# A fused attention and mixture-of-experts kernel: heads shifted by half a block, half maxima, and another order of the first loads

## The chip, the cores and the metric

The kernel runs on one core of a Trainium2 chip. The metric is device time in microseconds, the median of several executions. The core's engines work side by side, each through its own list of instructions in order, and wait for one another by semaphores: TensorE (PE, matmuls; PEld are its weight loads), VectorE (DVE), ScalarE (ACT), GpSimd (POOL) and SyncE (SP, which issues most transfers).

## What is computed

Two layers over eight images of 256 channels by 1024 pixels, all in float32. The part that the change touches is the attention of layer 0, with eight heads of 64 channels and a softmax over the queries (axis 1), not over the keys:

```python
qkv = (xt @ w_qkv + b_qkv).reshape(B, S, N_HEADS, 3 * D_K)
q, k, v = jnp.split(qkv, 3, axis=-1)
attn = jnp.einsum('bihd,bjhd->bijh', q, k) * SCALE
attn = jax.nn.softmax(attn, axis=1)
res = jnp.einsum('bijh,bjhd->bihd', attn, v).reshape(B, S, N_HEADS * D_K)
res = res @ w_out + b_out + xt
```

Layer 1 then normalizes the tokens, adds a second attention of one head over 256 channels, normalizes again, and adds a mixture of eight experts, of which each token uses the two best.

## The kernel before

**Stages.** The images are worked through one after the other. For each: `values` (v for all heads, tile pv, L260), `layer0` (projection of q and k, scores and sums, then the output projection pr, L345), `attend` (second attention) and `dispatch` (choice of experts; token rows are scattered into a DRAM table `rows`). The experts run once for images 0 to 6 as one group, ahead of image 7, and once for image 7 at the end. The results of the first group (`results`: gathers of the experts' rows, tile yk, weighted sums, transposes pout, output) are put between the head pairs of image 7.

**A step of layer 0.** Heads are taken in four pairs g, keys in eight blocks j of 128. For a step (g, j) `head_scores` computes, for both heads, a score tile psc of 128 keys by 1024 queries, in two matmuls of 512 queries each (L282). The contraction is over 64 channels, so that head 0 uses the upper and head 1 the lower 64 rows of the array. Keys lie on the partitions, so the softmax over queries runs along a row: DVE takes the negated maximum of 1024 elements (nmax, L287), ACT the exponential with its row sum (ex, sums, L289), DVE the reciprocal (rs, L294) and v scaled by it (vs, L296). `head_values` adds vs times ex into two sums po (L306), again with the two heads side by side. One profile record of a float32 matmul is half of it: a matmul has two records.

**What sets the order.** The kernel is written in a tile framework. A scheduler places the instructions on each engine and adds the semaphore waits that the reads and writes of tiles call for. Score tiles, projections and transposes share one pool of three PSUM buffers of 128 x 1024 (`ps_big`); the sums and other small results share two of 128 x 512 (`ps_acc`). The sums of step j come after the scores of step j + 1. The projections of a pair (pqk, L241, evicted by DVE at L249) stand ahead of its first step.

**Loads.** SP loads w_qkv as six transfers that put q, k and v apart, in runs of 64 elements (L89), then the first image (L81), the biases and w_out, then fills `rows` with zeros (L491, eight transfers of 8 MB). POOL's queue loads three small weights and copies the experts' weights into one packed table `wpack` in DRAM (L164 to L175). The image b + 1 is loaded when image b begins.

Of the kernel before, what the change touches and what calls it, by code (L numbers as in the profile page):

```python
# [10 lines left out]
F32 = mybir.dt.float32  # L11
I32 = mybir.dt.int32
AF = mybir.ActivationFunctionType
ALU = mybir.AluOpType
# [4 lines left out]
def kernel(  # L19
# [41 lines left out]
    one = ctx.enter_context(tc.tile_pool(name="one", bufs=1))  # L61
    two = ctx.enter_context(tc.tile_pool(name="two", bufs=2))
    four = ctx.enter_context(tc.tile_pool(name="four", bufs=4))
    small = ctx.enter_context(tc.tile_pool(name="small", bufs=6))
    rowp = ctx.enter_context(tc.tile_pool(name="rowp", bufs=3))
    keep = ctx.enter_context(tc.tile_pool(name="keep", bufs=8))
# [12 lines left out]
    def load_x(b):  # L79
        xT = two.tile([P, NCC, S], F32, tag="xT", name=f"xT_{b}")  # L80
        nc.sync.dma_start(xT, x[b].rearrange("(cc p) s -> p cc s", p=P))  # L81
        return xT


    wqkv = const.tile([P, NCC, 3, INNER], F32, name="wqkv")
    w_src = w_qkv.rearrange("(cc p) (h t d) -> p cc t h d", p=P, t=3, d=DK)
    for t in range(3):
        for cc in range(NCC):
            nc.sync.dma_start(  # L89
                wqkv[:, cc, t, :].rearrange("p (h d) -> p h d", d=DK), w_src[:, cc, t]  # L90
            )
    next_x = load_x(0)
    b_src = b_qkv.rearrange("(h t d) -> t h d", t=3, d=DK)
    b_rows = two.tile([NPAIR, 2, P], F32, tag="xb", name="b_rows")
    for t in range(2):
# [57 lines left out]
    later = const.tile([P, E, NT], F32, name="later")  # L153
    nc.gpsimd.memset(later, 1.0)
    nc.gpsimd.memset(later[:, :, 0:1], 0.0)
    zero = one.tile([P, 2 * D], F32, tag="n", name="zero")
    nc.gpsimd.memset(zero, 0.0)

    wpack = dram.tile([E * P, WROW], F32, name="wpack")
    wp = wpack.rearrange("(e p) c -> e p c", p=P)
    for dc in range(NCC):
        nc.gpsimd.dma_start(  # L164
            wp[:, :, ts(dc, FF)], w1.rearrange("e (dc p) f -> dc e p f", p=P)[dc]
        )
    for fc in range(NFC):
        at = NCC * FF
        nc.gpsimd.dma_start(
            wp[:, :, at + fc * D : at + (fc + 1) * D],  # L170
            w2.rearrange("e (fc p) d -> fc e p d", p=P)[fc],
        )
    at = NCC * FF + NFC * D + NFC
    for e in range(E):
        nc.gpsimd.dma_start(wp[e, :, at : at + D], b2[e].partition_broadcast(P))  # L175
    wbs = [const.tile([P, WROW], F32, name=f"wb_{i}") for i in range(NWB)]


# [14 lines left out]
    for dc in range(NCC):  # L193
# [4 lines left out]
    nc.tensor.transpose(ps[:, : E * NFC], b1_rows, ident[: E * NFC, : E * NFC])  # L198
    b1T = const.tile([P, E * NFC], F32, name="b1T")
    nc.vector.tensor_copy(b1T, ps[:, : E * NFC])  # L200
    at = NCC * FF + NFC * D
    nc.sync.dma_start(
        wpack.rearrange("(e p) c -> p e c", p=P)[:, :, at : at + NFC],
        b1T.rearrange("p (e fc) -> p e fc", fc=NFC),
    )

    def bcast(t, n):

# [18 lines left out]
    def to_channels(t, dst, name):  # L227

        for cc in range(NCC):
# [2 lines left out]
                nc.tensor.transpose(pt[:, ts(i, P)], t[:, i, ts(cc, P)], ident)  # L232
            nc.vector.tensor_copy(dst[:, cc, :], pt)


    def project(b, xT, g, t):

        pq = big(f"pqk_{b}_{g}_{t}")
        for cc in range(NCC):
            for n in range(NH2):  # L240
                nc.tensor.matmul(  # L241
                    pq[:, ts(n, 512)],
                    wqkv[:, cc, t, ts(g, P)],
                    xT[:, cc, ts(n, 512)],
                    start=(cc == 0),
                    stop=(cc == NCC - 1),
                )
        dst = two.tile([P, S], F32, tag=f"qk{t}", name=f"qk{t}_{b}_{g}")
        nc.vector.tensor_scalar(  # L249
            dst, pq, b_qk[:, t, g : g + 1], SCALE if t == 0 else 1.0, ALU.add, ALU.mult  # L250
        )
        return dst
# [15 lines left out]
                nc.vector.tensor_add(v[:, i + j, :], pv[:, ts(j, 512)], b_v)  # L268
        return v

    def head_scores(b, g, j, q, k, v):


        sums = small.tile([P, 2], F32, tag="sums", name=f"sums_{b}_{g}_{j}")
        exps = []
        pss = []
        for h in range(2):
            pss.append(big(f"psc_{b}_{g}_{j}_{h}"))
        for n in range(NH2):
            for h in range(2):  # L280
                r = slice(h * DK, (h + 1) * DK)
                nc.tensor.matmul(  # L282
                    pss[h][:, ts(n, 512)], k[r, ts(j, P)], q[r, ts(n, 512)], start=True, stop=True
                )
        for h in range(2):
            nmax = small.tile([P, 1], F32, tag="nmax", name=f"nmax_{b}_{g}_{j}_{h}")
            nc.vector.tensor_reduce(nmax, pss[h], AX.X, ALU.max, negate=True)  # L287
            ex = four.tile([P, 1024], F32, tag="exps", name=f"ex_{b}_{g}_{j}_{h}")
            nc.scalar.activation(  # L289
                ex, pss[h], AF.Exp, bias=nmax, scale=1.0, accum_out=sums[:, h : h + 1]  # L290
            )
            exps.append(ex)
        rs = small.tile([P, 2], F32, tag="rs", name=f"rs_{b}_{g}_{j}")
        nc.vector.reciprocal(rs, sums)  # L294
        vs = four.tile([P, 2, DK], F32, tag="vs", name=f"vs_{b}_{g}_{j}")
        nc.vector.tensor_mul(  # L296
            vs,
            v[:, j, ts(g, P)].rearrange("p (h d) -> p h d", d=DK),
            rs.unsqueeze(2).to_broadcast([P, 2, DK]),
        )  # L300
        return exps, vs

    def head_values(j, exps, vs, po):
        for n in range(NH2):
            for h in range(2):
                nc.tensor.matmul(  # L306
                    po[n][h * DK : (h + 1) * DK, :],
                    vs[:, h, :],
                    exps[h][:, ts(n, 512)],
                    start=(j == 0),  # L310
                    stop=(j == NT - 1),
                )

    def layer0(b, xT, between):
        v = values(b, xT)
        res = one.tile([P, NPAIR, S], F32, tag="res", name=f"res_{b}")
        pending = None

        def finish(g, j, exps, vs, po):
            head_values(j, exps, vs, po)  # L320
            if j == NT - 1:
                for n in range(NH2):
                    nc.scalar.copy(res[:, g, ts(n, 512)], po[n])

        for g in range(NPAIR):
            q = project(b, xT, g, 0)
            k = project(b, xT, g, 1)
            po = None
            for j in range(NT):
                exps, vs = head_scores(b, g, j, q, k, v)  # L330
                if pending is not None:
                    finish(*pending)
                if po is None:
                    po = [acc(f"po_{b}_{g}_{n}") for n in range(NH2)]
                pending = (g, j, exps, vs, po)
            for group, item in between[g]:
                results(group, [item])
        finish(*pending)


        t1 = one.tile([P, NT, C], F32, tag="t1", name=f"t1_{b}")
        for i in range(NT):
            pr = acc(f"pr_{b}_{i}")
            for g in range(NPAIR):
                nc.tensor.matmul(  # L345
                    pr[:, :C], res[:, g, ts(i, P)], wo[:, g, :], start=(g == 0), stop=False
                )
            for cc in range(NCC):
                nc.tensor.matmul(
                    pr[:, ts(cc, P)], xT[:, cc, ts(i, P)], ident, start=False, stop=(cc == NCC - 1)  # L350
                )
            nc.vector.tensor_add(t1[:, i, :], pr[:, :C], b_o)
        return t1


    def attend(b, t1):
# [20 lines left out]
        def scores(i):  # L377
            psc = big(f"ps1_{b}_{i}")
            for ec in range(NCC):
                for n in range(NH2):  # L380
                    nc.tensor.matmul(  # L381
                        psc[:, ts(n, 512)],
                        xa[:, ec, ts(i, P)],
                        nT[:, ec, ts(n, 512)],
                        start=(ec == 0),
                        stop=(ec == NCC - 1),
                    )
            nmax = small.tile([P, 1], F32, tag="nmax", name=f"nmax1_{b}_{i}")
            nc.vector.tensor_reduce(nmax, psc, AX.X, ALU.max, negate=True)  # L389
            ex = four.tile([P, 1024], F32, tag="exps", name=f"ex1_{b}_{i}")  # L390
            ssum = small.tile([P, 1], F32, tag="ssum", name=f"ssum_{b}_{i}")
            nc.scalar.activation(ex, psc, AF.Exp, bias=nmax, scale=1.0, accum_out=ssum)  # L392
            return ex, ssum
# [81 lines left out]
    class Group:  # L475


        def __init__(self, n, items):
# [7 lines left out]
            self.counts = None  # L486
            self.kept = {}

            per = E * self.cap // (2 * P)
            for c in range(0, per, 32):  # L490
                nc.sync.dma_start(  # L491
                    self.rows.rearrange("(p c r) d -> p c (r d)", p=P, r=2)[:, c : c + 32],
                    zero.unsqueeze(1).to_broadcast([P, 32, 2 * D]),
                )

    def dispatch(b, t2, group):

# [271 lines left out]
                nc.scalar.copy(oT, pt)  # L769
                nc.sync.dma_start(out[b, ts(cc, P), :], oT)  # L770

    groups = [Group(n, items) for n, items in enumerate(GROUPS)]
    waiting = []
    for b in range(B):
        group = next(g for g in groups if b in g.items)
# [58 lines left out]
```

## Time and profile before

| quantity | value |
|---|---|
| runs | 3018.35 us median of 3 (3017.9 to 3022.67) |
| profiled execution, its own time | 3014.45 us |
| its span | 3012.4 us |
| mean granted clock of TensorE | 0.943 of full speed |
| q1, hardware queue | 123.62 MB |
| q0, software queue | 83.87 MB |

The profile page gives, for one execution, the busy time of each engine, its share of the span and its number of instructions; then the span in 40 slices of about 75 us, with PEclk for the clock that was granted to TensorE. The chain that ended last is followed back from the last instruction to what released each. In the groups, `out<-in` names the tiles, `xN` counts instructions, and the two numbers behind the bar are busy time and mean nanoseconds of one. In the timeline each row is start, length, engine, line and operation; the bracket at its end is the engine's idle time before it, and what ended it. A busy PE may still wait inside: the end of a matmul is modelled, and matmuls overlap.

### The profile page before, as it was taken

What the parts mean: (1) busy time and instruction counts of PE and PEld (TensorE: products, weight loads), DVE (VectorE), ACT (ScalarE), POOL (GpSimd) and SP (SyncE); (2) the same over time, 40 slices, a digit from 0 to 9 for tenths busy, and PEclk for the clock granted to TensorE, in tenths of its full rate; (3) what the DMA queues carried; (4) which work ended last, traced back from release to release, by engine and by line L of the source; (5) the groups of instructions that cost most, each with busy time, mean ns of one, the idle gap of its engine ahead of it and who ended that gap; (6) DMA issues with size and microseconds to landing.
All of it is one profiled execution on the core that took longest, in us unless ns stands there. A gap on an engine that the chain in (4) does not pass through costs nothing.

```text
span 3012.4 us, 26498 instructions
## 1 busy us (share of the span) xinstructions
PE 2698.4 (90%) x10049; PEld 1421.2 (47%) x10049; DVE 1476.6 (49%) x2662; ACT 843.1 (28%) x1448; POOL 451.4 (15%) x458
## 2 busy tenths in 40 slices
PE   5999899989998999899989999999679997778946
PEld 2336433653365336533553355335467773234534
DVE  2554555445645554555445544654523335555422
ACT  1451145114511441144114411442112112333101
POOL 1000200020002000200010001000144433441043
PEclk9999999999999999999999999999789998889967
DMA  9980100010001000000000000000055542332044
GB/s 318 386 323 14 42 1 0 15 42 1 1 14 39 4 1 14 35 8 1 14 32 11 0 15 28 14 1 1 29 175 184 185 137 71 118 118 68 0 157 159
DMA packets 92456, 209.19 MB, mean 69 GB/s; under 512 B 23504, under 2 KB 24168, under 8 KB 90280
## 3 DMA queue, kind: packets, MB, share of 16 engines
q1 hardware_dynamic: 59928, 123.62, 11.4%
q0 software_dynamic: 32400, 83.87, 9.0%
q8 instruction: 79, 1.29, 0.2%
q14 instruction: 49, 0.40, 0.0%
HBM read 113.22 MB, written 126.36 MB: 80 GB/s over the span
## 4 chain that ended last, share of the span: by engine, by line
PE 71%; issue 13%; DVE 6%; DMA 4%; ACT 4%; POOL 1%; SPq 0%; ACTq 0%; POOLq 0%; DVEq 0%
PE psc L282 18%; PE po L306 15%; PE py L403 8%; PE pqk L241 7%; PE ps L381 6%; PE pv L260 4%; PE pr L345 4%; PE pt_n L232 2%; PE px L366 2%; DMA yk<-y,yat 2%; PE pa L398 2%; ACT ex L289 1%; PE pe L718 1%; PE pl L427 1%; DVE nmax L287 1%
## 5 line engine op out<-in xcount | busy, mean ns | idle before, releaser
L289 ACT ACTIVATE ex<-psc,nmax 128x1024 f32<-128x1024 f32 x512 | 570.3, 1115 | 706.3 <-DVE nmax L287 697.0
L282 PE MATMUL psc<-qk,qk 64*128 64x512 f32 x2048 | 654.7, 628 | 38.3 <-DVE qk L249 21.5
L287 DVE TENSOR_REDUCE nmax<-psc 128x1 f32<-128x1024 f32 x512 | 604.3, 1219 | 137.7 <-PE psc L282 130.9
L306 PE MATMUL po<-ex,vs 128*64 128x512 f32 x2048 | 530.1, 618 | 18.0 <-DVE vs L296 18.0
L282 PEld LDWEIGHTS psc<-qk,qk 64*128 64x128 f32 x2048 | 266.7, 189 | 417.4 <-issue 284.8
L567 POOL TENSOR_TENSOR t<-t,n 128x2048 f32<-128x2048 f32 x8 | 36.1, 4508 | 1980.0 <-issue 1559.9
L306 PEld LDWEIGHTS po<-ex,vs 128*64 128x64 f32 x2048 | 130.6, 138 | 384.9 <-issue 205.2
L403 PE MATMUL py<-n,aT 128*128 128x256 f32 x1024 | 236.5, 384 | 11.2 <-DVE aT L400 11.2
L241 PE MATMUL pqk<-xT,wqkv 128*128 128x512 f32 x512 | 239.6, 618 | 2.3 <-DVE qk L249 2.3
L381 PE MATMUL ps<-nT,xa 128*128 128x512 f32 x512 | 236.8, 592 | 0.0
L403 PEld LDWEIGHTS py<-n,aT 128*128 128x128 f32 x1024 | 190.4, 190 | 67.4 <-DVE aT L400 43.8
L294 DVE RECIPROCAL rs<-sums 128x2 f32<-128x2 f32 x256 | 42.1, 165 | 288.1 <-ACT ex L289 287.8
L260 PE MATMUL pv<-wqkv,xT 128*128 128x512 f32 x256 | 139.0, 695 | 32.5 <-DMA xT<-in_x_dram 32.5
L718 PE MATMUL pe<-wb,hb 128*128 128x256 f32 x624 | 155.2, 392 | 13.6 <-ACT hb L703 13.4
L392 ACT ACTIVATE ex<-ps,nmax 128x1024 f32<-128x1024 f32 x64 | 71.3, 1114 | 332.7 <-DVE nmax L389 325.0
L241 PEld LDWEIGHTS pqk<-xT,wqkv 128*128 128x128 f32 x512 | 97.6, 197 | 127.2 <-issue 124.2
L693 PE MATMUL ph<-xb,wb 128*128 128x256 f32 x624 | 151.7, 386 | 3.1 <-DVE xb L685 3.1
L560 POOL DMA_INDIRECT rows<-n,d_at x128 | 124.9, 976 | 180.3 <-DVE row L547 128.4
L750 POOL DMA_INDIRECT yk<-y,yat x128 | 123.4, 964 | 179.0 <-DVE o L756 117.4
L703 ACT ACTIVATE hb<-ph,wb 128x256 f32<-128x256 f32 x156 | 65.5, 471 | 283.9 <-issue 237.6
L408 DVE SCALAR_TENSOR_TENSOR t<-py,rs,t 128x256 f32<-128x256 f32 x64 | 30.9, 483 | 228.2 <-PE py L403 228.2
L249 DVE TENSOR_SCALAR qk<-pqk,b_qk 128x1024 f32<-128x1024 f32 x64 | 82.1, 1283 | 119.7 <-PE pqk L241 119.7
(151 smaller groups left out, 2374.6 us busy)
## 6 DMA issues: line engine op xcount, KB each, us to landing
rows<-zero SPq DMA_DIRECT2D x8, 8192.0 KB, 51.1
y<-yb SPq DMA_DIRECT2D x78, 256.0 KB, 2.3
xT<-in_x_dram SPq DMA_DIRECT2D x8, 1024.0 KB, 5.1
sums<-t SPq DMA_DIRECT2D x8, 1024.0 KB, 3.9
o<-sums SPq DMA_DIRECT2D x8, 1024.0 KB, 6.7
out_dram<-oT SPq DMA_DIRECT2D x16, 512.0 KB, 7.6
wpack<-in_L_ffn_w_dram POOLq DMA_DIRECT2D x4, 1024.0 KB, 19.2
rows<-n,d_at POOLq DMA_INDIRECT x128, 2.4
```

The source lines that it names most:

```text
L241: nc.tensor.matmul(pq[:, ts(n, 512)], wqkv[:, cc, t, ts(g, P)], xT[:, cc, ts(n, 512)], start=(cc == 0), stop=(cc == NCC - 1),)
L260: nc.tensor.matmul(pv[:, ts(j, 512)], xT[:, cc, ts(i + j, P)], wqkv[:, cc, 2, :], start=(cc == 0), stop=(cc == NCC - 1),)
L282: nc.tensor.matmul(pss[h][:, ts(n, 512)], k[r, ts(j, P)], q[r, ts(n, 512)], start=True, stop=True)
L287: nc.vector.tensor_reduce(nmax, pss[h], AX.X, ALU.max, negate=True)
L289: nc.scalar.activation(ex, pss[h], AF.Exp, bias=nmax, scale=1.0, accum_out=sums[:, h : h + 1])
L306: nc.tensor.matmul(po[n][h * DK : (h + 1) * DK, :], vs[:, h, :], exps[h][:, ts(n, 512)], start=(j == 0), stop=(j == NT - 1),)
L381: nc.tensor.matmul(psc[:, ts(n, 512)], xa[:, ec, ts(i, P)], nT[:, ec, ts(n, 512)], start=(ec == 0), stop=(ec == NCC - 1),)
L403: nc.tensor.matmul(py[:, :D], aT[:, ts(m, P)], n1[:, m, :], start=(m == 0), stop=(m == NT - 1))
L560: nc.gpsimd.indirect_dma_start(out=view[:, :], out_offset=bass.IndirectOffsetOnAxis(ap=at[:, i : i + 1], axis=0), in_=n2[:, i, :], in_offs ...
L693: nc.tensor.matmul(ph[:, ts(fc, BR)], wb[:, dc * FF + fc * P : dc * FF + (fc + 1) * P], xb[:, dc, :], start=(dc == 0), stop=(dc == NCC - 1),)
L718: nc.tensor.matmul(py[:, ts(r, D)], hT[:, fc, ts(r, P)], wb[:, at + fc * D : at + (fc + 1) * D], start=(fc == 0), stop=(fc == NFC - 1),)
L750: nc.gpsimd.indirect_dma_start(out=yk[:, :], out_offset=None, in_=group.y[:, :], in_offset=bass.IndirectOffsetOnAxis(ap=ats[k][:, i : i + ...
```

## The change

Five edits go together.

1. **Order of the steps.** The steps of all four pairs form one list of 32. In an iteration, PE takes the first half of head 0 of this step, then the second half of head 1 of the step before, then the second half of head 0, then the first half of head 1. The sums follow two steps behind (`LAG = 2`). The exponentials get a pool of six buffers of their own.
2. **Maxima in halves.** The maximum of the first 512 queries is taken when these are there. For the other 512 an instruction multiplies by -1, takes the minimum with the first result and accumulates the minimum over the row; its full output goes into a tile `scrap` that nobody reads.
3. **Projections.** Those of the next pair are put behind steps 3 and 5 of the present pair.
4. **First loads.** The first image and w_qkv are loaded first, in whole rows, by four transfers; six copies on ACT and DVE then put q, k and v apart.
5. **Zeros and packed weights.** The zero fills and the copies into `wpack` all go through SP, behind the first k eviction. The zeros come from a DVE memset of a buffer that the experts use later.

```diff
-        for h in range(2):
-            nmax = small.tile([P, 1], F32, tag="nmax", name=f"nmax_{b}_{g}_{j}_{h}")
-            nc.vector.tensor_reduce(nmax, pss[h], AX.X, ALU.max, negate=True)
...
+        def first_max(at, h):
+            g, j = steps[at]
+            nmax = small.tile([P, 1], F32, tag="nmax1", name=f"nmax1_{b}_{g}_{j}_{h}")
+            nc.vector.tensor_reduce(nmax, pss[at, h][:, ts(0, 512)], AX.X, ALU.max, negate=True)
+            nmaxes[at, h] = nmax
+        def soften(at, h):
...
+            nc.vector.tensor_scalar(
+                scrap, ps[:, ts(1, 512)], -1.0, nmaxes.pop((at, h)),
+                ALU.mult, ALU.min, accum_out=nmax,
+            )
+            ex = expp.tile([P, 1024], F32, tag="exps", name=f"ex_{b}_{g}_{j}_{h}")
+            nc.scalar.activation(
+                ex, ps, AF.Exp, bias=nmax, scale=1.0, accum_out=sums[at][:, h : h + 1]
+            )
...
+        for at in range(last + LAG + 1):
+            if at <= last:
+                score(at, 0, 0)
+            if 0 < at <= last + 1:
+                score(at - 1, 1, 1)
+                soften(at - 1, 1)
+            if at <= last:
+                first_max(at, 0)
+                score(at, 0, 1)
+                score(at, 1, 0)
+                soften(at, 0)
+                first_max(at, 1)
+            if at >= LAG:
+                gather_values(at - LAG)
+            if at <= last:
+                g, j = steps[at]
+                if j == NT - 1:
+                    for group, item in between[g]:
+                        results(group, [item])
+                if g + 1 < NPAIR and j in (3, 5):
+                    if j == 3:
+                        qks.append([])
+                    qks[g + 1].append(project(b, xT, g + 1, len(qks[g + 1])))
```

`score(at, h, n)` is the matmul of L282 for head h and half n; `gather_values` is the former `head_values` with the copy of finished sums. The loads:

```diff
-    for t in range(3):
-        for cc in range(NCC):
-            nc.sync.dma_start(
-                wqkv[:, cc, t, :].rearrange("p (h d) -> p h d", d=DK), w_src[:, cc, t]
-            )
-    next_x = load_x(0)
+    for cc in range(NCC):
+        nc.sync.dma_start(next_x[:, cc, :], x[0, ts(cc, P), :])
+        nc.sync.dma_start(w_raw[:, cc, :], w_qkv[ts(cc, P), :])
+    for t in (2, 0, 1):
+        for cc in range(NCC):
+            copy = nc.scalar.copy if cc == 0 else nc.vector.tensor_copy
...
+    def prepare():
+        zero = wbs[0][:, : 2 * D]
+        with tc.issue_after(evicted[0, 0, 1].ins):
+            nc.vector.memset(zero, 0.0)
...
+        first = fill(groups[0])[0]
+        with tc.issue_after(first.ins):
+            pack()
+            for group in groups[1:]:
+                fill(group)
```

## The prediction

> **What bounds the kernel now.** I read the engine totals first, then the clock slices, the chain that ended last, the costly groups, and at last the timeline of one step of the convolution attention.
>
> ```profile
> span 3012.4 us, 26498 instructions
> ...
> PE 2698.4 (90%) x10049; PEld 1421.2 (47%) x10049; DVE 1476.6 (49%) x2662; ACT 843.1 (28%) x1448; POOL 451.4 (15%) x458
> ...
> PE psc L282 18%; PE po L306 15%; PE py L403 8%; PE pqk L241 7%; PE ps L381 6%; PE pv L260 4%; PE pr L345 4%; PE pt_n L232 2%; PE px L366 2%; DMA yk<-y,yat 2%; PE pa L398 2%; ACT ex L289 1%; PE pe L718 1%; PE pl L427 1%; DVE nmax L287 1%
> ```
>
> TensorE (PE) looks busy 90% of the span, and the two groups that the change rebuilds, the scores psc and the sums po, lead the chain. "Busy" hides small stalls, though, so I look at the pieces of the chain:
>
> ```profile
> 422.30 2.22 PE psc L282 x8
> 424.53 1.87 PE po L306 x8
> 426.39 2.42 PE psc L282 x7
> 428.81 1.87 PE po L306 x8
> ...
> 439.05 7.06 PE pqk L241 x16
> 446.11 1.86 PE po L306 x6
> 447.98 1.92 PE psc L282 x8
> ```
>
> A step is one psc block (4 matmuls, 8 records, the two heads side by side in the array) and one po block. With no stall it takes 1.92 + 1.87 = 3.79 us; in the steady state two steps take 2.22 + 1.87 + 2.42 + 1.87 = 8.38, so 4.19 each. What sets the 4.19 is the timeline's ring through two engines:
>
> ```profile
> 126.28 0.29 DVE L296 TENSOR_TENSOR vs<-v,rs 128x128 f32<-128x128 f32 x1
> 126.49 2.35 DVE L287 TENSOR_REDUCE nmax<-psc 128x1 f32<-128x1024 f32 x2
> ...
> 127.80 1.11 ACT L289 ACTIVATE ex<-psc,nmax 128x1024 f32<-128x1024 f32 x1 [1.75 <-DVE nmax L287]
> ...
> 128.93 1.11 ACT L289 ACTIVATE ex<-psc,nmax 128x1024 f32<-128x1024 f32 x1
> ...
> 130.17 0.17 DVE L294 RECIPROCAL rs<-sums 128x2 f32<-128x2 f32 x1 [1.33 <-ACT ex L289]
> 130.37 0.29 DVE L296 TENSOR_TENSOR vs<-v,rs 128x128 f32<-128x128 f32 x1
> 130.76 2.36 DVE L287 TENSOR_REDUCE nmax<-psc 128x1 f32<-128x1024 f32 x2
> ```
>
> max, exp, exp, reciprocal, scaled v, next max: DVE idles 1.33 us in front of rs. Stalled time to be won is thus 0.40 us in most steps, plus about 2 us at each change of head pair (psc piece of 3.76). In image 1 this stage runs from the projection at 353.5 to the first pr at 528.8: 175.3 us.
>
> **The change: the new step.** Lag 2 and the half-block shift break that ring: rs and vs are needed only a step later. But the built program's order shows a new wait. On PE a step is now: A = [head 0, first half, step s; head 1, second half, step s-1], B = [head 0, second half, s; head 1, first half, s], then po of s-2. The first matmul of B waits for DVE, for the half-maximum of the first half of the same score tile, although it writes the other half. Queued behind it on PE are B's second matmul and all of po; on DVE the second-half maxima wait for them. I price this ring from rows of before:
>
> - A: first pass to second, 0.53 (first psc block: weight loads at 57.79, 58.32, 58.75, 59.18).
> - Last pass to the start of the maximum: 59.81 - 59.18 = 0.63.
> - The half-maximum: L287 takes 1.219 for 1024 elements, L443 0.225 for 64, about 1.04 ns per element, so 0.69 for 512.
> - DVE end to PE start: 0.06 (L249 starts 56.45, takes 1.28; psc at 57.79).
> - B: 0.53 to its second pass, and from the last pass to po 0.53 (an unstalled block is 1.92, its last pass starts after 1.39).
> - po to the next block: 1.87.
>
> Sum 4.84 us. It would be 3.79 without the wait. Break-even comes below.
>
> What else could set the step? DVE: first max starts at A+1.16; head 1's min-accumulate at A+1.8; head 0's after B, at A+3.07; then the other first max, rs, vs. With the min-accumulate at S us the next first max (A+6.0) is late only if 3.07 + S + 0.63 + 0.5 > 6.0, S > 1.8. No row shows S: L268 (512 elements out of PSUM) is 0.68, L249 (1024, same instruction without the accumulator) 1.28. Below 0.68 nothing changes either, since the ring does not run through it; I take 0.75, the form of L249 at half length. ScalarE: two exps end about A+5.06, and B of the next step needs one at A+6.7. Both covered; if the cover went, the step would grow by the excess.
>
> The Trainium skill (VectorE: DVE Perf Modes, "Two Vector instructions with no wait between them") says that an op that also writes its accumulator is two instructions. For DVE no row shows it, for ScalarE one does: ACTIVATION_READ_ACCUMULATOR, 194 ns. By it S would be near 0.95 and the sum the same.
>
> **Projections** move out of the pair change, to after steps 3 and 5. Each is half of 7.06, 3.53, plus 0.08 for one more block change. In the next step DVE evicts first (1.28), so first max starts 0.15 later: 3.76 each. Pair change stalls go.
>
> One image: first pair's projections and eviction 7.06 + 1.43; two steps without po to fill the pipe about 6.8; 30 x 4.84 = 145.2; 6 x 3.76 = 22.6; at the end a last half score, max, exp, rs, vs and po, about 5.8. Sum 188.9, against 175.3: **+13.6 us an image**. Seven images +95. In image 7 the results of the first seven lie between the pairs, and 31.8 us pass from the first pout (2541.0) to the next psc (2572.8), of which gathers, not PE, set most. The projection leaves that hole and two score steps come in, of about its length; I take +14 there too, bounded by 0 (the scores hide fully) and +35 (7 us of projection at three pair changes now uncovered, on top).
>
> **Head.**
>
> ```profile
> 0.81 6.78 SPq L89 DMA_DIRECT2D wqkv<-in_L_conv_w_qkv_dram  x6
> ...
> 32.48 2.04 PE L260 MATMUL pv<-wqkv,xT 128*128 128x512 f32 x2 [32.48 <-DMA xT<-in_x_dram]
> ```
>
> The first real matmul waits for xT while the copies into wpack (POOL's queue) and wqkv in pieces of 256 B share the DMA engines: xT, 1 MB, took 24.7 us to land here, 5.1 in the median. Now x and w_qkv go first, in whole rows, and the wpack copies move behind. 2.5 MB at 1 MB per 5.1 us is 12.8, plus 0.8 to issue, plus a copy of at most 0.69 (as L268) before the last operand: 14.3. Bounds: 2 us faster (three landings overlap), or 6 slower if the small packets of W_rows, b_v and wo stand between. **-18**, range -12 to -20. Six w copies on ACT and DVE: two of them on the path, counted; the others lie under pv's 17 us. On SP the x of image 1 is now ahead of the zero fills; the fills start after the first k eviction, near 40 us instead of 31.5, and the twelve small wpack transfers, off POOL's queue, come behind seven of them. The fills took until about 215 us (slices of 386, 323, then 14 GB/s), and the first scatter comes after 348: some 100 us of cover; without it the scatter would wait. The zeroing moves to DVE, one instruction of about 0.5 us, under psc. Six exps buffers, the renamed tags and Group's move cost nothing: no wait on them is listed.
>
> **Sum.** Profiled execution 3014.45 + 95 + 14 - 18 = 3105.5. That execution is 3.9 below the median of 3018.35, so against the median runs I say **3109 us**.
>
> **Rivals.**
>
> 1. *The half waits hide, faster.* If the wait for the first max were met by the time PE gets to B, the step is bounded by the score buffers: first max, min, exp, exp end at A+4.9 and free the buffer for the next B, which gives about 3.9. Image: 188.9 - 30 x 0.94 = 160.7, all -117 - 18: 2883. For it: PE's order is free in the other waits, and DVE is only half busy. Against: the wait is in the program, and nothing is queued between A and B to fill it. It decides from a step below 4.84 - (109 - 18)/240 = 4.46. Chance 0.08.
> 2. *A slow accumulate, slower.* S of 2.2 would make DVE the bound: 2 x 2.2 + 1.8 = 6.2 a step, 256 x 1.36 more: 3457. Against: L249 at twice the length is 1.28. Chance 0.02.
> 3. *The clock.* PE now idles some 0.8 us in each step. In the windows view PE was busy 170.9 of 175.2 us in image 1's stage at a clock of 0.99, and 49.4 of 65 at 0.87 in image 7 (2560 to 2625), with gaps of microseconds. At 0.87, 3.79 of PE time per step becomes 4.36: 256 x 0.57 = 146 more, 3255. Chance 0.05.
> 4. *Image 7 overlaps better, or the edits move stages less than I think*: 3010 to 3047, or within 0.2%. Chance 0.05, of which 0.02 no change.
>
> The skill (TensorE: Matmul & The Clock Gate, "A second HAM failure mode") reports a kernel whose micro-idles in a PSUM-cycling loop lost clock, which speaks for 3; its "HAM oscillation" section asks for gaps over 3.4 us, which speaks against. By the one 3255, by the other 3109; nothing here with gaps below 1 us shows a loss.
>
> **Numbers.** Forecast 3109: 0.80. Its range: +-0.1 us per step (a half-maximum of 0.6 to 0.8) is +-26, fill, tail and projections +-2 an image +-16, head and image 7 +-20, all added: 3047 to 3171, which leaves out the rivals' 0.2. What a measurement of this kernel can tell from no change is about 0.2%. Faster 0.08, same 0.02, slower 0.90.
>
> **What would show it.** Right: PE idle in front of the score matmuls released by DVE's first max, some 0.7 to 0.8 us, about 250 times; step 4.8; pr of image 1 about 189 us after its first projection; no 1.33 us idle in front of rs; first pv near 8, the second near 14. Wrong: steps of 3.9 with the idle gone (1), DVE without idle (2), granted clock below 0.95 in image 1's stage (3).

## The result and the profile after

The changed kernel takes 3134.24 us (median of 4 runs, 3129.54 to 3136.67) against 3018.12 of before beside it: ratio 1.039, 95% interval 1.0356 to 1.0424. It is slower by 3.9%. Its profiled execution has a span of 3135.0 us, 122.6 more than before.

From the page of the changed kernel: the span, the engine totals, and the costly groups of the stage (busy time and mean ns behind the bar, then idle time just before the group, its cause, and that cause's part).

```profile
span 3135.0 us, 27735 instructions
...
PE 2718.0 (87%) x10049; PEld 1342.0 (43%) x10049; DVE 1555.2 (50%) x3690; ACT 860.7 (27%) x1451; POOL 442.1 (14%) x445
...
L324 PE MATMUL psc<-qk,qk 64*128 64x512 f32 x2048 | 691.5, 685 | 194.1 <-DVE nmax L332 154.0
L377 PE MATMUL po<-ex,vs 128*64 128x512 f32 x2048 | 517.4, 622 | 9.6 <-DVE vs L361 9.6
L332 DVE TENSOR_REDUCE nmax<-psc 128x1 f32<-128x512 f32 x512 | 351.7, 689 | 264.7 <-PE psc L324 264.3
L324 PEld LDWEIGHTS psc<-qk,qk 64*128 64x128 f32 x2048 | 197.7, 196 | 660.4 <-DVE nmax L332 356.1
L342 DVE TENSOR_SCALAR_CACHE_REDUCE scrap<-psc,nmax 128x512 f32<-128x512 f32 x512 | 382.1, 746 | 161.9 <-PE psc L324 161.8
```

PE works 20 us more, but its share falls from 90% to 87%: the time went into waits. Matmuls and weight loads of the scores wait for DVE's first maximum. Before, the long waits of the ring were DVE's for the exponential (rs, 287.8 us in 222 times in the waits view); 14.7 us in 11 times are left of these. DVE got 1028 more instructions and is still only half busy. The chain of this page breaks off early (it explains a tenth of the span), so I read the steps from the timeline.

One step of image 1 in the timeline of the changed kernel (start, length, engine, line, operation; the bracket is the idle time before it):

```profile
401.59 1.13 PE L324 MATMUL psc<-qk,qk 64*128 64x512 f32 x4
402.75 0.69 DVE L332 TENSOR_REDUCE nmax<-psc 128x1 f32<-128x512 f32 x1 [1.64 <-PE psc L324]
403.36 0.74 DVE L342 TENSOR_SCALAR_CACHE_REDUCE scrap<-psc,nmax 128x512 f32<-128x512 f32 x1
...
403.49 1.13 PE L324 MATMUL psc<-qk,qk 64*128 64x512 f32 x4 [0.78 <-DVE nmax L332]
404.02 0.08 DVE L342 DVE_READ_ACCUMULATOR scrap<-psc,nmax 128x1 f32 x1
...
404.55 1.94 PE L377 MATMUL po<-ex,vs 128*64 128x512 f32 x8
...
406.42 1.13 PE L324 MATMUL psc<-qk,qk 64*128 64x512 f32 x4
```

A at 401.59, the first maximum at 402.75, B only at 403.49 after 0.78 us of idle PE, the sums at 404.55, the next A at 406.42: 4.83 us a step. The built program shows which instruction holds B. These are its rows for A and B of one step on PE (tile name: image, pair, key block, head):

```
L324 Matmult psc_4_1_7_0 128x512 [waits Activation]
L324 Matmult psc_4_1_6_1 128x512 [waits DVE]
L324 Matmult psc_4_1_7_0 128x512 [waits DVE]
L324 Matmult psc_4_1_7_1 128x512 [waits Activation]
```

The third row is the second half of head 0's tile. It reads the same q and k tiles as the first row, which does not wait for DVE. What DVE has just done is to read the *first* half of the tile that it writes: the row waits for the count that this maximum sets. (The second row waits for DVE too, for head 1's first maximum of the step before, which is over by then.)

### The profile page after: what moved, and what is told of

It reads as the page before. It is cut to its first block, busy times and chain, and to the rows that moved or that the text cites. A ratio compares the mean times of both kernels' runs of the same rounds, so it can differ in the third digit from the quotient of the medians.

```text
span 3135.0 us, 27735 instructions
## 1 busy us (share of the span) xinstructions
PE 2718.0 (87%) x10049; PEld 1342.0 (43%) x10049; DVE 1555.2 (50%) x3690; ACT 860.7 (27%) x1451; POOL 442.1 (14%) x445
## 5 line engine op out<-in xcount | busy, mean ns | idle before, releaser
L324 PE MATMUL psc<-qk,qk 64*128 64x512 f32 x2048 | 691.5, 685 | 194.1 <-DVE nmax L332 154.0
L377 PE MATMUL po<-ex,vs 128*64 128x512 f32 x2048 | 517.4, 622 | 9.6 <-DVE vs L361 9.6
L332 DVE TENSOR_REDUCE nmax<-psc 128x1 f32<-128x512 f32 x512 | 351.7, 689 | 264.7 <-PE psc L324 264.3
L324 PEld LDWEIGHTS psc<-qk,qk 64*128 64x128 f32 x2048 | 197.7, 196 | 660.4 <-DVE nmax L332 356.1
L342 DVE TENSOR_SCALAR_CACHE_REDUCE scrap<-psc,nmax 128x512 f32<-128x512 f32 x512 | 382.1, 746 | 161.9 <-PE psc L324 161.8
L786 PE MATMUL pe<-wb,hb 128*128 128x256 f32 x624 | 155.2, 392 | 13.6 <-ACT hb L771 13.4
```

What stands on the lines that cost most here:

```text
L324: nc.tensor.matmul(pss[at, h][:, ts(n, 512)], k[r, ts(j, P)], q[r, ts(n, 512)], start=True, stop=True)
L332: nc.vector.tensor_reduce(nmax, pss[at, h][:, ts(0, 512)], AX.X, ALU.max, negate=True)
L342: nc.vector.tensor_scalar(scrap, ps[:, ts(1, 512)], -1.0, nmaxes.pop((at, h)), ALU.mult, ALU.min, accum_out=nmax,)
L377: nc.tensor.matmul(po[n][h * DK : (h + 1) * DK, :], vs[:, h, :], exs[h][:, ts(n, 512)], start=(j == 0), stop=(j == NT - 1),)
L786: nc.tensor.matmul(py[:, ts(r, D)], hT[:, fc, ts(r, P)], wb[:, at + fc * D : at + (fc + 1) * D], start=(fc == 0), stop=(fc == NFC - 1),)
```

## The experiments

Ratios are to the kernel before on the same chip, which stood at 3014 to 3050 us in these jobs. Times of the stage of image 1 run from its first projection to its first pr: 175.4 us before, 193.4 in the changed kernel.

### whole_max: the new order with the old maximum

```diff
...
-            nc.vector.tensor_reduce(nmax, pss[at, h][:, ts(0, 512)], AX.X, ALU.max, negate=True)
...
-            nc.vector.tensor_scalar(
-                scrap, ps[:, ts(1, 512)], -1.0, nmaxes.pop((at, h)),
-                ALU.mult, ALU.min, accum_out=nmax,
-            )
+            nc.vector.tensor_reduce(nmax, ps, AX.X, ALU.max, negate=True)
```

> The changed kernel with one maximum over all 1024 queries per head instead of two halves; order of steps, lag, projections and loads as changed. Theory (the wait of the second-half matmul on the first half's maximum costs the time): the wait is gone, the next bound is the score buffers, max, exp, exp, about 3.9 us a step instead of 4.82, so about 230 us less, some 2880 to 2910. Rival A (the new order itself, half a block apart and two steps late, is what costs): a step stays near 4.8 and the time above 3080. Rival B (the extra instructions of the halves on VectorE cost): also faster, but no TensorE idle should have been released by the maximum; told apart by the run with halves taken later.

Measured: 2902.66 us, ratio 0.9591 (0.9561 to 0.962). Two steps in its timeline:

```profile
400.49 2.04 PE L324 MATMUL psc<-qk,qk 64*128 64x512 f32 x8
...
401.67 2.36 DVE L340 TENSOR_REDUCE nmax<-psc 128x1 f32<-128x1024 f32 x2 [1.20 <-PE psc L324]
402.46 1.94 PE L367 MATMUL po<-ex,vs 128*64 128x512 f32 x8
...
404.33 2.17 PE L324 MATMUL psc<-qk,qk 64*128 64x512 f32 x8
```

A and B are one block again. This step takes 3.84 us; over image 1 the steps without a projection take 3.78 to 4.02, near the 3.79 that PE needs. The stage of image 1 falls to 164.4 us. So the order, the lag, the projections and the loads come with a gain of 4.1%, and the half maxima alone turn that into a loss: 0.080 of the time of before, some 240 us, or 0.94 for each of 256 steps on average.

Not all of this lies in the steps. From the first pv of an image to its first projection of q the two kernels run the same instructions, yet over images 1 to 6 this takes 135.4 us in the changed kernel, 134.3 before and 111.5 in whole_max. The granted clock there is 0.79 to 0.81 in the first two and 0.91 to 1.00 in whole_max (in image 4, 22.58 us at 0.79 against 18.14 at 1.00). That is 24 of the 234 us between the spans of whole_max and the changed kernel, and 23 of the 111 between whole_max and before. Why the clock differs there, no run shows, so these parts can't be put down to the order or to the half maxima.

### max_after: half maxima, but behind both halves

Both instructions for the maximum stay; the first is only written behind the matmul of the second half.

```diff
-                first_max(at, 0)
                 score(at, 0, 1)
                 score(at, 1, 0)
+                first_max(at, 0)
                 soften(at, 0)
-                first_max(at, 1)
```

(and `first_max(at - 1, 1)` ahead of `soften(at - 1, 1)`.)

> The changed kernel with both half-maximum instructions kept, but the first one stands behind both score matmuls of its tile, so that nothing on TensorE has to wait for it. Theory: the wait is gone though all VectorE instructions are there; first max, min-accumulate, first max, min-accumulate, exp, exp run one behind the other, step about 4.1 us, time 2930 to 2970. Rival A (order costs) and rival B (the extra VectorE instructions cost): step stays at 4.6 to 4.8, time above 3070.

Measured: 2958.18 us, 0.9783 (0.9751 to 0.9814); steps without a projection take 3.9 to 4.4 us, 4.2 in the mean, and no wait of the scores for DVE's maximum is left. DVE does the same instructions as in the changed kernel, so their number costs no more than 0.019 of the time here (some 58 us, against whole_max). The other three quarters of the 240 us came back when the first maximum moved: 18 of these 180 us lie in the v projections at another clock, the rest is the wait.

### po_between: the sums into the gap

The wait seems to ask for work between A and B, so the sums are put there: `gather_values(at - LAG)` moves up.

```diff
                 first_max(at, 0)
+            if at >= LAG:
+                gather_values(at - LAG)
+            if at <= last:
                 score(at, 0, 1)
                 score(at, 1, 0)
                 soften(at, 0)
                 first_max(at, 1)
-            if at >= LAG:
-                gather_values(at - LAG)
```

> The changed kernel with the four sum matmuls of step s-2 placed between the first and the second pair of score matmuls, that is into the gap in which TensorE waits for the first maximum. Rival (the gap can just be filled): step 3.9 us, time near 2890. Theory with the ring worked through: the second half of head 1 then follows its first half at once and waits for that one's maximum, which stands on VectorE behind the min-accumulate of head 0 (0.63 + 0.65 + 0.69 + 0.05 us): the step grows to 5.2 to 5.5 us, time 3220 to 3310.

Measured: 3232.13 us, 1.0682 (1.0639 to 1.0725). Its timeline on PE:

```profile
439.55 1.94 PE L377 MATMUL po<-ex,vs 128*64 128x512 f32 x8
441.42 2.21 PE L324 MATMUL psc<-qk,qk 64*128 64x512 f32 x6
444.31 1.12 PE L324 MATMUL psc<-qk,qk 64*128 64x512 f32 x2 [0.68 <-DVE nmax L332]
445.36 1.94 PE L377 MATMUL po<-ex,vs 128*64 128x512 f32 x8
```

B and the next A now stand back to back, and the wait moves to the end of that block: the second half of head 1 waits for head 1's first maximum, which DVE takes late. From sums to sums it is 5.81 us here, in a step between two projections, and 5.5 in most others. Filling one wait moved it to the other head.

### halves_only: the old order, half maxima alone

```diff
+            if n == 0:
+                for h in range(2):
...
+                    nc.vector.tensor_reduce(
+                        first, pss[h][:, ts(0, 512)], AX.X, ALU.max, negate=True
+                    )
...
-            nc.vector.tensor_reduce(nmax, pss[h], AX.X, ALU.max, negate=True)
+            nc.vector.tensor_scalar(
+                scrap, pss[h][:, ts(1, 512)], -1.0, firsts[h], ALU.mult, ALU.min, accum_out=nmax
+            )
```

> The kernel before with the maxima taken in two halves and nothing else. Theory: the second-half matmuls wait for the first maxima here too, one score block now holds 0.63 + 0.69 + 0.05 us of waiting for head 0 and another 0.6 us for head 1, and the ring max, exp, exp, rs, vs stays, so a step of 5.0 to 5.3 us instead of 4.19; 256 steps make 3220 to 3310. Rival (halves are harmless by themselves and cost only with the shifted heads): within 1% of the kernel before.

Measured: 3518.3 us, 1.1636 (1.1601 to 1.1672). The direction was right, the size was missed by over 200 us. One step on PE:

```profile
445.63 1.13 PE L284 MATMUL psc<-qk,qk 64*128 64x512 f32 x4
447.54 1.12 PE L284 MATMUL psc<-qk,qk 64*128 64x512 f32 x2 [0.78 <-DVE nmax L290]
448.59 1.07 PE L317 MATMUL po<-ex,vs 128*64 128x512 f32 x2
449.60 1.12 PE L284 MATMUL psc<-qk,qk 64*128 64x512 f32 x2
450.65 1.93 PE L317 MATMUL po<-ex,vs 128*64 128x512 f32 x6
452.51 1.13 PE L284 MATMUL psc<-qk,qk 64*128 64x512 f32 x4
```

The same 0.78 us is there, but two more losses. The second halves of the heads wait for two maxima that end 1.0 us apart, with the reciprocal and the scaled v between them on DVE, and the scheduler put a matmul of the sums between them. A matmul of one head alone (x2, two records) holds PE for 1.05 us, as long as a pair of both heads (404.55 - 403.49 = 1.06 for the x4 of the changed kernel's step above). So 1.05 for the scores and 1.0 for the sums are paid twice: 1.91 + 1.05 + 1.01 + 1.05 + 1.86 = 6.88. The Trainium skill (TensorE: Matmul & The Clock Gate, "Part 3: Packing small matmuls — row/col tiling") says that matmuls on different row groups run at the same time in the array; here two heads in one block cost what one costs alone. The shift by half a block in the change keeps a half of each head in every block.

### block_tiles and reads_first: is it the tile?

If B waits because it shares a tile with the first maximum, another tile should free it. block_tiles gives each *block* a tile in place of each head: head 0's half in the left columns, head 1's half in the right. PE's order stays. The exponential becomes two instructions, and DVE adds the two row sums.

```diff
-            if n == 0:
-                pss[at, h] = big(f"psc_{b}_{g}_{j}_{h}")
+            if h == 0:
+                tiles[at, n] = big(f"psc_{b}_{g}_{j}_{n}")
+            at_tile = (at, n) if h == 0 else (at + n, 1 - n)
...
+            half = tiles[at_tile][:, ts(h, 512)]
...
+            for n in range(NH2):
+                nc.scalar.activation(
+                    ex[:, ts(n, 512)], pss[at, h, n], AF.Exp, bias=nmax, scale=1.0,
+                    accum_out=sums[at][:, n, h : h + 1],
+                )
...
+                nc.vector.tensor_add(rs, both[:, 0, :], both[:, 1, :])
```

> The changed kernel with the same order of matmuls and the same half maxima, but each score tile now holds one block of PE (head 0's half in its first 512 columns, head 1's half in its last 512) in place of both halves of one head. So the first half of a head and its second half lie in two tiles, and B writes a tile that the first maximum does not read. ScalarE takes the exponential in two instructions of 512, and DVE adds their two row sums, one more small instruction in a step. Theory (the wait comes from the tile, not from the place: B is held because first and second half share one tile): the 0.78 us of PE idle in front of B, released by DVE's maximum, goes, the step falls from 4.83 to between 3.8 and 4.3 us, and 256 steps give 140 to 260 us: 2870 to 3000. Rival (B is held by the maximum itself, or by DVE's load of half maxima, accumulator reads and small instructions, whichever tile they use): the idle stays, step 4.8 or more, 3100 to 3180. Third way: the four exponentials of a step make ScalarE the bound, PE idles in front of po or of A released by ScalarE, step 4.4 to 4.8, 3020 to 3110.

Measured: 3432.42 us, 1.1293 (1.1259 to 1.1326). The wait that I meant to remove is gone: no wait of the scores for DVE's maximum is listed. But the time is far from all three expectations. The waits view and the timeline show why:

```profile
PEld psc L329 <- ACT ex L349: 408.0, 387, 2.8
DVE nmax L336 <- ACT ex L349: 310.8, 226, 1.6
```

```profile
436.23 0.68 ACT L349 ACTIVATE ex<-psc,nmax 128x512 f32<-128x512 f32 x1
...
437.03 0.69 DVE L336 TENSOR_REDUCE nmax<-psc 128x1 f32<-128x512 f32 x1 [1.37 <-ACT ex L349]
...
437.84 0.75 DVE L344 TENSOR_SCALAR_CACHE_REDUCE scrap<-psc,nmax 128x512 f32<-128x512 f32 x1
...
438.70 0.69 ACT L349 ACTIVATE ex<-psc,nmax 128x512 f32<-128x512 f32 x1 [1.70 <-DVE scrap L344]
```

DVE's first maximum of head 1 waits for ScalarE's exponential of head 0. It needs nothing from it. They only read the left and the right of one tile, and the program puts even these two *reads* in order. Maximum, minimum, exponential, next maximum have become one chain through two engines. So the second kernel writes both of DVE's reads of a tile ahead of the exponentials that read it, and changes nothing else:

```diff
                 score(at, 0, 1)
                 score(at, 1, 0)
-                soften(at, 0)
-                first_max(at, 1)
+                lower(at, 0)
+                first_max(at, 1)
+                soften(at, 0)
```

(`lower` is the minimum of `soften`; likewise `lower(at - 1, 1)` and `first_max(at, 0)` ahead of `soften(at - 1, 1)`.)

> block_tiles with one thing moved: of each score tile, both reads of DVE (the first maximum of one head and the minimum of the other) are now written ahead of the exponentials that read the same tile. In block_tiles the program let DVE's first maximum of one head wait for ScalarE's exponential of the other head, a read behind a read in the same tile, and that wait closed a ring of its own. Theory (two instructions on one tile are put in order by the tile, whatever columns they take, and that wait is what block_tiles paid): DVE's maximum no longer waits for ScalarE, B does not wait for DVE, the step falls to between 3.9 and 4.6 us and the kernel to between 2890 and 3080, below the changed kernel's 3134. Rival (half maxima with exponentials in halves are too much work for DVE and ScalarE, about 3.6 and 3.0 us in a step by the rows of block_tiles, with the waits between them): step 5 or more, 3180 to 3430.

Measured: 2930.0 us, 0.9687 (0.9659 to 0.9715): 500 us less than block_tiles by the order of its lines alone, and 200 less than the changed kernel. Its timeline on PE:

```profile
349.15 1.99 PE L329 MATMUL psc<-qk,qk 64*128 64x512 f32 x8
351.07 1.94 PE L381 MATMUL po<-ex,vs 128*64 128x512 f32 x8
352.94 3.70 PE L273 MATMUL pqk<-xT,wqkv 128*128 128x512 f32 x8
```

A and B run through, and this step takes 352.94 - 349.15 = 3.79 us with every half maximum in its place. That settles the cause: neither the half maxima nor their number holds B, but a tile that is read in one half and written in the other. Even so it is 0.0096 behind whole_max. With the wait gone, the half maxima have nothing left to win, since PE is the bound; nor is it shown that they cost anything: of the 19 us between the two profiled spans, 17 lie in the v projections of images 1 to 6 (128.3 against 111.5 us, four of the six at a clock of 0.79 or 0.80), which are the same in both.

### loads_only: the old loop with the new head

Parts 4 and 5 of the change on the loop of before; the six buffers of the exponentials stay too.

> The kernel before with the new first loads, the copies, the zero fills and packed weights behind the first k eviction, and nothing else. Theory: the start of the first projection moves from 49.4 to about 29.3 us and nothing else, so 20 us less, 2996 to 3000. Rival (the fills and the packed weights, now later, run into the first image): less than 10 us gained.

Measured: 3003.54 us, 0.9931 (0.9905 to 0.9958), a gain of 0.7%. The first projection starts at 27.1 us in place of 49.4, the first pr 23.9 earlier, but the pr of image 6 only 15.8 earlier and the span is 14.3 shorter. Part of the head's gain is given back later, at about 1.4 us an image. It goes in the stage of layer 0, which takes 177.4 to 182.9 us in images 1 to 6 against 175.4 before. In images 1 to 3 one or two of the first steps are longer; in image 2 PE idles 3.06 us before the scores at 654.32, released by an exponential. Why, I did not settle; the six buffers are a candidate as well as the loads and fills.

### warm_fill: PE kept busy at the start of each image

In the first two steps of an image, where no sums are due, two more matmuls per step, whose result nobody reads:

```diff
+            else:
+                idle = acc(f"idle_{b}_{at}")
+                for n in range(NH2):
+                    nc.tensor.matmul(
+                        idle, wqkv[:, 0, 0, ts(0, P)], xT[:, 0, ts(n, 512)], start=True, stop=True
+                    )
```

> The changed kernel with two more matmuls of 512 columns, whose result nobody reads, in each of the first two steps of every image, where no sums stand yet: some 3.4 us more of TensorE work an image. Theory (the 4 to 5 us an image that the sum missed are a half clock of 13.7 us after a thin start): the half-clock window shrinks to one or two of 3.4 us, the first sums come no later than before, and the time falls by 15 to 35 us to 3100 to 3120. Rival (the fill is long by its chain alone): the clock stays low for 13.7 us or the fill grows by the work, time 3134 to 3165.

Measured: 3129.97 us, 1.0348 (1.0318 to 1.0378), against 1.0356 to 1.0424 for the changed kernel: the intervals overlap, no gain is shown. The windows view from the first scores of image 1 on (length, busy time of PE, PEld, DVE, ACT and POOL with their counts, granted clock, DMA share, GB/s), the changed kernel first:

```profile
358.20:385.00 26.80, 24.10 (x59) 7.85 (x60) 13.09 (x30) 8.44 (x14) 9.19 (x10) 0.75 0.15 51
```

```profile
354.60:381.50 26.90, 21.62 (x65) 7.00 (x64) 13.27 (x31) 8.43 (x14) 8.91 (x10) 0.94 0.14 49
```

The added matmuls raised the clock, 0.94 in place of 0.75, and the same stretch is as long as before. Their time is not the reason: those of the first step run ahead of this stretch, from 352.83, and with those of the second PE is still busy 2.5 us less. It idles 2.6 us more, in one wait that the changed kernel does not have here:

```profile
362.78 1.13 PE L324 MATMUL psc<-qk,qk 64*128 64x512 f32 x4
366.54 2.08 PE L324 MATMUL psc<-qk,qk 64*128 64x512 f32 x4 [2.62 <-DVE nmax L332]
```

DVE begins that maximum late, after 3.56 us of idle whose releaser the profile does not name ("remote"). From the first scores to the first sums the images 1 to 6 take 13.5 to 15.9 us, against 13.4 to 13.6 in the changed kernel. So the run does not tell what the low clock alone costs. The 4 us by which its median is lower are not the fill's: in the profiled execution the v projections of images 1 to 6 are 8 us shorter.

### late_projections and values_in_fill: two steps beyond whole_max

late_projections is whole_max with image 7's projections back at the change of pairs, behind the results. values_in_fill is whole_max with the v projection of images 1 to 7 moved into the first two steps.

```diff
+                if g + 1 < NPAIR and between[g] and j == NT - 1:
+                    qks.append([project(b, xT, g + 1, t) for t in range(2)])
-                if g + 1 < NPAIR and j in (3, 5):
+                if g + 1 < NPAIR and not between[g] and j in (3, 5):
```

```diff
             if at >= LAG:
                 gather_values(at - LAG)
+            elif b > 0:
+                values(b, xT, v, ((0, 2), (4, 6))[at])
```

> The kernel with the whole maximum (2902.7 us) with the projections of image 7, and only those, put back to the change of pairs, behind the results. Theory (the results' gathers set the time of a pair change there, and the projections that lay in that hole are now outside it): image 7 shortens by 10 to 20 us, time 2883 to 2893. Rival (what moved into the hole is worth as much as what left it): within 4 us of 2902.7.

> The kernel with the whole maximum with the v projection of images 1 to 7 put into the first two steps of the image, where the sums are missing and TensorE waits for the first softmax. Theory: 9.2 us from the first scores to the first sums hold only about 5 us of matmuls, so 4 us an image come back, 20 to 35 us in all, time 2868 to 2883. Rival (the v tiles take two of the three score buffers and VectorE's time, and the first steps stall longer): 2900 or more.

late_projections: 2887.01 us, 0.9529 (0.9488 to 0.9571), the lowest median here, ahead of both kernels; its interval just overlaps that of whole_max (0.9561 to 0.962), so it is the trace that shows the gain. The stretch of image 7 from pv to pr falls from 296.1 in whole_max to 280.5 us: 15.6 us was the price of taking the projections out of the holes that the results leave. values_in_fill: 2915.74 us, 0.9646 (0.9617 to 0.9674), no gain over whole_max, where 2868 to 2883 had been expected; its images take some 290 us in place of 288. That idea falls.

## Why the prediction was right, and where its sizes were off

**The new wait** was the mechanism, and its price was right. A to B was put at 0.53 + 0.63 + 0.69 + 0.06 = 1.91; it is 1.90. The step was put at 4.84; it is 4.83. block_tiles and reads_first show that the shared tile makes it. PE's idle time in front of the scores, released by DVE's maximum, is 154.0 us in 196 times, not about 250: in a step behind a projection the wait before B is put down to DVE's eviction (0.32 us at 384.64), and such a step costs the 3.76 that were forecast.

**The accumulate** S was taken at 0.75. It is 0.74 plus a row of its own of 0.08. The Trainium skill (VectorE: DVE Perf Modes, "Two Vector instructions with no wait between them") counts such an op as two instructions; the trace agrees, but at 0.08 and not at ScalarE's 0.19. As forecast it is off the path: DVE idles before it, waiting for PE.

**The head** was put at -18 with the first pv near 8 and the second near 14. The changed kernel:

```profile
7.26 2.08 PE L292 MATMUL pv<-wqkv,xT 128*128 128x512 f32 x2 [7.26 <-ACT wqkv L95]
10.71 1.10 DVE L95 COPY wqkv<-w_raw 128x512 f32<-128x512 f32 x3 [5.80 <-DMA w_raw<-in_L_conv_w_qkv_dram]
11.19 2.08 PE L292 MATMUL pv<-wqkv,xT 128*128 128x512 f32 x2 [1.85 <-DVE wqkv L95]
```

The second operand came 2.8 us earlier than thought, and the first projection starts at 29.3 in place of 49.4: -20.1. Whether the loads and the fills delay nothing later stays open: loads_only gave part of the gain back, but the cause was not found.

**An image** was put at +13.6 us. From one image to the next it is 320.79 - 303.53 = +17.26, and from the first projection to pr +18.0. The term that was mis-sized is the fill, "two steps without po to fill the pipe about 6.8". With 2.97 for the third step up to its sums that makes 9.8 from the first scores to the first sums; the timeline of the changed kernel has 371.82 - 358.24 = 13.6:

```profile
358.24 1.13 PE L324 MATMUL psc<-qk,qk 64*128 64x512 f32 x4 [1.38 <-DVE qk L281]
360.15 3.65 PE L324 MATMUL psc<-qk,qk 64*128 64x512 f32 x6 [0.78 <-DVE nmax L332]
364.58 7.31 PE L324 MATMUL psc<-qk,qk 64*128 64x512 f32 x12 [0.79 <-DVE nmax L332]
371.82 2.98 PE L377 MATMUL po<-ex,vs 128*64 128x512 f32 x8
```

Twelve records take 7.31 us here, at a clock of 0.50, and 3.70 in whole_max's fill, at 1.00. So 3.8 of the missing 4.4 us per stage (18.0 - 13.6) lie in the fill, well outside the +-2 an image that the range allowed for it. Whole_max, whose fill has no wait for a first maximum, needs 334.19 - 324.98 = 9.2 in image 1, and 8.1 in images 2 to 6, where its clock is 1.00. That the clock alone makes the 3.8 is not shown, since warm_fill ran into another wait. The total still came within the range because that adds up the bounds of all terms, and the step, its largest, was met to 0.01 us.

**Rival 3, the clock**, was right in its worry and wrong in its place. In the steady steps nothing is lost (the changed kernel over image 1's whole stage and over steady steps of image 0, then before over image 1's stage):

```profile
349.80:543.20 193.40, 169.77 (x577) 50.80 (x575) 110.87 (x270) 80.57 (x135) 15.64 (x16) 0.96 0.03 11
146.00:220.00 74.00, 64.62 (x238) 18.36 (x234) 43.73 (x111) 34.20 (x58) 0.00 (x0) 1.00 0.86 300
```

```profile
353.30:528.70 175.40, 171.14 (x577) 60.82 (x575) 101.01 (x141) 78.68 (x135) 15.39 (x16) 0.99 0.04 13
```

From 146 to 220 us PE idles 9.4 of 74 us in gaps of 0.78, and the clock is 1.00. Image 1's stage has 0.96 against 0.99, and the loss is at its start (0.75 in the window above). The kernel before had it already: in its fill of image 1, from 361.73 to 369.45, the clock is 0.84 though PE idles only 0.90 us in it, behind a gap of 1.38. So the prediction's "nothing here with gaps below 1 us shows a loss" held for the steady steps and left this fill out. In the Trainium skill (TensorE: Matmul & The Clock Gate), the section "A second HAM failure mode: psum-queue depth-cycling", on micro-idles, fits the fill, where no idle row of PE is longer than 1.4 us; "HAM oscillation", which asks for gaps over 3.4 us, fits the steady steps. Neither says where the border between the two lies, and no run here shows it.

**Image 7** was put at +14, within 0 to +35; from pv to pr it is 308.05 - 282.50 = +25.5. I let the scores fill the holes that the projections leave. late_projections shows that, in whole_max, the projections cost 15.6 us outside those holes. There the stretch is 296.1 - 282.5 = 13.6 over before. The longer steps cost 25.5 - 13.6 = 11.9 more, out of the 30 that 32 steps of 0.94 would make: the holes seem to hide the other 18.

**The sum.** Head -20.1; image 0 +16.4, then six times 17.26, +120.0 together; from the pr of image 6 to the end +22.6: +122.5, the difference of the spans but for rounding. Forecast were -18, +95 and +14. The 32 us between the two are 25 from the first seven images, nearly all of it the fill, and 9 from image 7, less 2 from the head.

**Rivals 1, 2 and 4** did not come: the steps are 4.83, not 3.9; DVE idles; only the head was cheaper than thought, by 2 us. What rival 1 described, steps of about 3.9, is what whole_max reaches when the wait is taken away; reads_first reaches 3.79.

## What to carry to other kernels

A piece that is ready early gains nothing if the rest of its tile is still to be written: what a dependence covers in this framework is the tile, so read the waits in the built program, give the pieces tiles of their own, and write all reads of one engine ahead of those of the next. A gain is taken only where the engine of that wait is not the bound: here the new order without the split maximum brought PE within 0.1 us a step of its limit, and the split maximum had nothing left to give. Putting work into a gap can move the wait, as po_between did, and small matmuls that share the array should stay next to each other: apart, each pair cost 1 us more here. And before a difference is put down to an edit, see what its untouched stages did: here the v projections alone moved by up to 24 us with the clock.

## What the hardware showed that I had not expected

- In a fill with no idle row of PE above 1.4 us the granted clock fell to one half for about 14 us: it was 1.00 from 358 to 360, 0.58 from 360 to 362, 0.50 from 362 to 372, 0.51 from 372 to 374 and 1.00 from 374 to 378. In the 3.3 us before it fell, PE had idled 1.38 and 0.78. In the steady steps 0.78 us of idle in every 4.83 us left it at 1.00.
- The same v projections of one image take 18.1 us at a granted clock of 1.00 and 22.6 at 0.79, both in one execution of reads_first.
- A matmul over 64 rows and 512 columns in float32 holds PE for 1.05 us alone and for 1.06 together with its twin on the other 64 rows.
- DVE's accumulator read is a row of its own, 0.08 us; ScalarE's is 0.19.
